# Two tiles of h made together, one small tile moved to another pool, and x1's transposes placed inside root's products

## The chip, the cores and the metric

The kernel runs on one core of a Trainium2 chip. The metric is the device time of one execution in microseconds (us); the kernel before takes 970.1 us (median of three runs, 969.67 to 971.27). TensorE is called PE, VectorE DVE, ScalarE ACT, GpSimd POOL; SP is the engine whose queue issues nearly all of the DMAs.

## The reference

Two graph layers over N = 625 nodes with D = 1024 features and E = 20,000 edges of R = 8 types, all in float32:

```python
# layer 0: attention over edges
h = x @ W
al, ar = h @ a[0, :d], h @ a[0, d:]
e = exp(-leaky_relu(al[src] + ar[dst], 0.1))
hp = segment_sum(e[:, None] * h[dst], src) / (segment_sum(e, src)[:, None] + 1e-5)
x = layernorm(x + elu(hp))
# layer 1: relational convolution with a gate
u = x @ root + bias
for r in range(8):
    sums, cnt = segment_sum(msgs of type r, dst), segment_sum(mask of type r, dst)
    u = u + (sums / max(cnt, 1)) @ weight[r]
z = concat([u, x]) @ w_gate + b_gate
x = layernorm(x + tanh(u) * z + x * (1 - z))
```

## The kernel before

The nodes are cut into ST = 5 tiles of 125 rows, the features into KC = 8 chunks of 128 or two halves of 512. All of it lies in one function, `fast` (L523); its order of instructions on each engine comes from a scheduler that goes by the program's order and by when operands are ready, except where `in_turn` (L561) pins an instruction to its place in the program. PSUM has eight banks, six in pool 0 and two in pool 1 (`bank`, L554).

**Layer 0.** SP loads the edge lists, x tile 0, the eight chunks of W (`load_w0`, L566), and x tile 1. POOL stores the packed edges to DRAM. `x_turned` (L717) turns a tile of x by eight PE transposes (px, L680) and ACT copies it (xT, L721). `h_parts` (L784) makes one tile of h: for each chunk two products (ph, L789), one per half, and at the end two ACT copies (h_sb, L793). Between tile 0's chunks stand `gather_edges` (L742: six small PE products, p_count, L746 and L747, then DVE's block numbers L749 and L751, and POOL's two gathers L755) and `place_edges` (L759: two PE transposes, p_edges, L763, and four DVE instructions that give keys and sources).

Then comes the counts stage. `one_hots` (L806, instructions L815) lets DVE compare keys and sources with a ramp; up to HOTS = 5 bundles of one-hots are held. For each of 55 groups `counts_of` multiplies them on PE (pc, L839) and ACT casts the counts (cj, L844); SP stores a tile's counts to DRAM (L900). The groups are interleaved with h of tiles 1 to 4 as steps of one chunk: 32 steps over the first H_GROUPS = 38 groups. A list `due` says after which group other work is issued: `row_sums` (L796, DVE's products L800, the attention's al and ar), `counted`, and `first_scores`, which begins with `spread_ar` (PE's p_ar, L930; ACT's copy L932). After the last group come the scores on DVE (L870 to L883), their transposes (patt, L891) and the products att times h (phh, L691). `attend` (L1089 on) makes x1 of a tile: elu, layernorm (scaled by ACT, L1111) and a store.

**Layer 1.** A float32 product is made of three: weights are cut into pieces g, m, e by ACT and DVE (`prepare`, L1014), x1 into pieces h, l, d (`turned_pieces`, L1040: eight transposes px, L680, then ACT L1035 and DVE L1036, L1037). `dense` (L1068) runs a weight half over the five tiles; in `dense_tiles` (L1045) a tile has sixteen first products (g times h L1051, m times l L1052) and eight second ones (e times d, L1055). For tile 0, and where two tiles go together, the second ones lie between the first ones; otherwise they follow. The two tiles 3 and 4 go together in root0 and root1. root0 is the first pass: after tile t's results are put, `later_x1(t)` calls `attend(t + 3)` and `turned_pieces(t + 2)`.

For each type r and half, `dense` gives y = x1 times weight, kept as two pieces in tiles of the pool f_y, and the neighbours' sum is 50 products pu (L1249): a 125 x 128 block of counts cf as weights, a piece of y with 512 columns moving. That makes 800 pu products in 16 blocks. `use_ins` (L1187) and `sum_ins` (L1196) use one small tile, in_p, 125 x 1, to check the number of edges; it lies in f_y behind inv, ahead of the y tiles. Layout in bytes of a partition: y tiles at 48,928 and on (288 modulo 512, each 2,048 long), cf at 77,184 (384 modulo 512). The pieces g, m, e, h, l, d are all at 384 modulo 512.

Of the kernel before, what the change touches and what calls it, by code (L numbers as in the profile page):

```python
# [10 lines left out]
F32 = mybir.dt.float32  # L11
# [11 lines left out]
KC = D // 128  # L23
# [417 lines left out]
ST = 5  # L441
TN = N // ST
# [80 lines left out]
def fast(  # L523
# [39 lines left out]
        tc.keep_in_program_order(ins)  # L563


    def load_w0(wpool):  # L566

        chunks = []
        for k in range(KC):
            if k % 2:  # L570
                w = rawp.tile([128, 2, HALF], F32, tag="raw", name=f"w0_{k}").rearrange("p i c -> p (i c)")
            else:
                w = wpool.tile([128, D], F32, tag="w", name=f"w0_{k}")
            nc.sync.dma_start(w, w0[k * 128:(k + 1) * 128, :])
            chunks.append(w)
        return chunks

    def load_row(rows, ap, name):
# [83 lines left out]
    def load_x(pool, t, name, bufs=None, eng=nc.sync, clear=False):  # L662

        xt = pool.tile([128, D], F32, tag="x", name=f"{name}_{t}", bufs=bufs)
        if t < ST - 1:
            eng.dma_start(xt, x[t * TN:t * TN + 128, :])
        else:
            if clear:
                nc.gpsimd.memset(xt[96:], 0.0)
            xr = x[t * TN:t * TN + rows_of(t), :]  # L670
            move_rows(rows_of(t), lambda rows: eng.dma_start(xt[rows], xr[rows]))
        return xt

    def transposed(src_t, n, name, put, pool=None):

        for g in range(2):
            p = bank(f"{name}_{g}", pool)
            for j in range(4):
                k = 4 * g + j
                nc.tensor.transpose(p[:, j * 128:j * 128 + n], src_t[:n, k * 128:(k + 1) * 128], ident[:n, :n])  # L680
            put(slice(4 * g, 4 * g + 4), p.rearrange("q (j n) -> q j n", j=4)[:, :, :n])

    banks_h = {}
# [11 lines left out]
    with tc.tile_pool(name="f_w", bufs=4, side="right") as wpool, \  # L695
# [10 lines left out]
        for i, ap in ((1, dst), (0, src), (2, etype)):  # L706
            nc.sync.dma_start(edge_rows[:, i, :], ap.rearrange("(p c) -> p c", c=per))
            if i == 1:
                x_next = load_x(xin, 0, "x")
        w0_sb = load_w0(wpool)  # L710
        nc.gpsimd.dma_start(packed[0:1, :], pad[:, :BLOCK])
        nc.gpsimd.dma_start(packed[NBLOCK + 1:, :].rearrange("(o i) c -> o (i c)", o=1), pad)
        x_next = [x_next, load_x(xin, 1, "x")]
        al_row = load_row(scores, a[0, :D], "al_row")
        ar_row = load_row(scores, a[0, D:], "ar_row")

        def x_turned(t):  # L717
            n = rows_of(t)
            xt = x_next.pop(0)
            xT = xin.tile([128, KC, 128], F32, tag="xT", name=f"xT_{t}")  # L720
            transposed(xt, n, f"px_{t}", lambda ks, p: nc.scalar.copy(xT[:, ks, :n], p), 0)  # L721
            if t + 2 < ST:
                x_next.append(load_x(xin, t + 2, "x"))
            return xT
# [17 lines left out]
        def gather_edges():  # L742

            p = bank("p_count", 0)
            for m in range(per // BLOCK):
                nc.tensor.matmul(p[:2 * NGS, :1], less[:, m, :], ones16[:TN], start=m == 0, stop=False)  # L746
            nc.tensor.matmul(p[:2 * NGS, :1], ahead16.rearrange("p g h -> p (g h)"), ones16[:1], start=False, stop=True)  # L747
            base = scores.tile([2 * NGS, 1], F32, name="base")
            nc.vector.tensor_copy(base, p[:2 * NGS, :1])  # L749
            at_block = scores.tile([2 * NGS, 2, 4], I32, name="at_block")  # L750
            nc.vector.tensor_scalar(at_block, later[:2 * NGS], base, float(NBLOCK + 1), op0=OP.add, op1=OP.min)  # L751
            edges = scores.tile([2 * NGS, 2, 4, BLOCK], F32, name="edges")
            for b in range(2):

                nc.gpsimd.indirect_dma_start(edges[:, b].rearrange("p i c -> p (i c)"), None, packed[:, :],  # L755
                                             bass.IndirectOffsetOnAxis(ap=at_block[:, b, :1], axis=0))
            return edges
# [25 lines left out]

        def h_parts(t, xT):  # L784
            n = rows_of(t)
            halves_h = [bank(f"ph_{t}_{half}", 1) for half in range(2)]
            for k in range(KC):
                for half, p in enumerate(halves_h):
                    nc.tensor.matmul(p[:n, :], xT[:, k, :n], w0_sb[k][:, half * HALF:(half + 1) * HALF],  # L789
                                     start=k == 0, stop=k == KC - 1)  # L790
                if k == KC - 1:
                    for half, p in enumerate(halves_h):
                        nc.scalar.copy(h_sb[:n, t, half * HALF:(half + 1) * HALF], p[:n, :])  # L793
                yield
# [104 lines left out]
            for r in range(R):  # L899
                nc.sync.dma_start(cd[r][:, :, j * 128:(j + 1) * 128], cj[:, :, r, :])  # L900

        for k, _ in enumerate(h_parts(0, xT_next)):
            if k == 0:
                edges = gather_edges()
            if k == KC - 2:
                place_edges()
        due = [(LAG, row_sums, 0)]
        cjs = []
        es = []

        def other_h():
            xT = x_turned(1)
            yield
            for t in range(1, ST):
                for k, _ in enumerate(h_parts(t, xT)):
                    if k == KC // 2 and t + 1 < ST:
                        xT_after = x_turned(t + 1)
                    yield
                xT = xT_after

        h_steps = other_h()
        next(h_steps)
        n_steps = (ST - 1) * KC
        steps = 0

        def spread_ar():
# [22 lines left out]
        for i in range(NGS):  # L949
            while steps < min(n_steps, (i + 1) * n_steps // H_GROUPS):  # L950
                next(h_steps, None)
                steps += 1
                if steps % KC == 0:
                    due.append((i + (LAG if steps < n_steps else 0), row_sums, steps // KC))
                    if steps == n_steps:
                        due.append((i + 6, first_scores, None))
            if i % NG == 0:
                cj = cjp.tile([128, ST, R, 128], F16, tag="cj", name=f"cj_{i // NG}")
                nc.gpsimd.memset(cj[:, :, :, TN:], 0.0)
                cjs.append(cj)  # L960
            n = built[i][2]
            if i == builds[n][0] and n + HOTS - 1 < len(builds):
                one_hots(n + HOTS - 1)
            counts_of(i, cjs[-1])
            if i % NG == NG - 1:
                due.append((i + LAG, counted, i // NG))
            due.sort(key=lambda d: d[0])
            while due and due[0][0] <= i:
                _, do, arg = due.pop(0)
                do(arg)  # L970
# [71 lines left out]
        h, l, d = x1[t] = [xp.tile([128, KC, 128], F32R, tag=f"{i}_{t}", name=f"{name}_{i}_{t}") for i in "hld"]  # L1042
        transposed(src_t, 128, f"p{name}_{t}", lambda ks, p: pieces_of(h, l, d, ks, p))

    def dense_tiles(ts, chunks, name, by_chunk):  # L1045

        sums = {t: (bank(f"p1_{name}_{t}"), bank(f"p2_{name}_{t}")) for t in ts}

        def first(t, k, g, m):
            h, l, _ = x1[t]  # L1050
            nc.tensor.matmul(sums[t][0], h[:, k, :], g, start=k == 0, stop=False, skip_group_check=True)  # L1051
            nc.tensor.matmul(sums[t][0], l[:, k, :], m, start=False, stop=k == KC - 1, skip_group_check=True)  # L1052

        def second(t, k, e):
            nc.tensor.matmul(sums[t][1], x1[t][2][:, k, :], e, start=k == 0, stop=k == KC - 1, skip_group_check=True)  # L1055

        for k, (g, m, e) in enumerate(chunks):
            for t in ts:
                first(t, k, g, m)
                if by_chunk:  # L1060
                    second(t, k, e)
        if not by_chunk:
            for k, (g, m, e) in enumerate(chunks):
                for t in ts:
                    second(t, k, e)
        return sums

    def dense(name, put, after=None, goes_on=False, whole=False):  # L1068

        chunks = [ready.pop(0) for _ in range(KC)]  # L1070


        steps = [(t,) for t in range(ST - 2)] + ([(ST - 2, ST - 1)] if goes_on else [(ST - 2,), (ST - 1,)])
        for ts in steps:
            for t, (p1, p2) in dense_tiles(ts, chunks, name, ts[0] == 0 or len(ts) > 1).items():
                n = 128 if whole else rows_of(t)
                put(t, p1[:n, :], p2[:n, :])
                if t == 1:
                    prepare(UNITS - KC)
                if after:  # L1080
                    after(t)
        prepare(2 * KC - UNITS)
# [78 lines left out]
                done.append(attend(t + 3))  # L1161
            turned_pieces(done[t + 2], t + 2, "x1")

    dense("root0", start_u(0), after=later_x1, goes_on=True, whole=True)
    elus.close()

    yp = ctx.enter_context(tc.tile_pool(name="f_y", bufs=1))
# [14 lines left out]
        for t in range(2, ST):  # L1182
            nc.vector.tensor_tensor(ins, ins16[:, t, :], ins, op=OP.add)

    in_p = yp.tile([TN, 1], F32, name="in_p")

    def use_ins():  # L1187
        p = bank("p_ins")
# [175 lines left out]
```

## Time and profile before

| what | before |
|---|---|
| runs | 970.1 us median (969.67 to 971.27) |
| profiled execution | 969.78 us, its span 968.0 us |
| granted PE clock | 0.995 of full speed on average |
| DVE, ACT, POOL busy | 596.6, 405.6, 36.5 us |
| PE px of x tile 0 | starts at 5.02 |
| first product of h | starts at 8.69 |
| first one-hot on DVE (L815) | 24.81 |
| last row sum on DVE ends | 104.08 |
| first phh | 111.14 |

The span runs from the first to the last instruction of the profiled execution; the remainder of its own time lies around it. A row of a timeline gives start, duration, engine, line and operation, output and inputs, the number of instructions joined in the row, and in brackets the idle time before them with what ended it. A row of PE's products counts the last one to its end, so that a row's duration is longer than the distance to the next row; the pitch is that distance over the number of products. Float32 products such as ph show two records each; pieces in the rounded form fp32r show one.

### The profile page before, as it was taken

To read this page: it belongs to the slowest core of one execution; us is meant where nothing else is said; L and a number is where in the kernel's file an instruction comes from. 1 tells how busy PE (TensorE), PEld (TensorE's weight loads), DVE (VectorE), ACT (ScalarE), POOL (GpSimd) and SP (SyncE) were. 2 spreads that over 40 slices of the span, in tenths; PEclk is the share of its full clock that TensorE was granted. 3 is DMA by queue.
4 is the path that set the end of the run, shared out by engine and by line. 5 is a ranking of instruction groups with operands and counts; after the bars stand their busy time and mean duration, and the time that the engine had idled before them with its cause. 6 is when DMAs were issued, how large, how long until landed. Compare 5 with 4: busy or idle time off the path is not lost.

```text
span 968.0 us, 10885 instructions
## 1 busy us (share of the span) xinstructions
PE 945.6 (98%) x4075; PEld 730.1 (75%) x4075; DVE 596.6 (62%) x964; ACT 405.6 (42%) x732; POOL 36.5 (4%) x59
## 2 busy tenths in 40 slices
PE   7999999999999999999999999999999999999994
PEld 3555546788888888888888888888888888888883
DVE  1998899853645737536356265363562654668996
ACT  1333857652452444415515434345243451435322
POOL 3000001000000000000000000000000000001123
PEclk9999999999999999999999999999999999999997
DMA  8123652341202213103021121220320211451213
GB/s 300 44 73 101 186 191 90 110 136 41 87 24 99 77 33 121 65 24 114 27 68 66 57 87 55 67 87 6 117 66 22 87 44 44 148 157 37 72 43 109
DMA packets 60479, 81.79 MB, mean 84 GB/s; under 512 B 29195, under 2 KB 29607, under 8 KB 60420
## 3 DMA queue, kind: packets, MB, share of 16 engines
q1 hardware_dynamic: 60212, 80.84, 26.3%
q8 instruction: 34, 0.56, 0.2%
q14 instruction: 25, 0.20, 0.1%
q0 software_dynamic: 208, 0.19, 0.1%
HBM read 69.26 MB, written 11.75 MB: 84 GB/s over the span
## 4 chain that ended last, share of the span: by engine, by line
PE 87%; DVE 8%; ACT 2%; issue 1%; POOL 1%; DMA 0%; SPq 0%; DVEq 0%; POOLq 0%; ACTq 0%
PE pu L1249 19%; PE p_w L1051 15%; PE p_w L1052 15%; PE p_w L1055 15%; PE ph L789 7%; PE p_wgx L1052 2%; PE p_wgx L1055 2%; PE p_wgx L1051 2%; PE pc L839 2%; PE p_root L1052 1%; PE p_root L1055 1%; PE p_root L1051 1%; PE p_wgu L1051 1%; PE p_wgu L1055 1%; PE p_wgu L1052 1%
## 5 line engine op out<-in xcount | busy, mean ns | idle before, releaser
L1051 PE MATMUL p_w<-g_w,x_h 128*128 128x512 f32 x640 | 249.2, 389 | 0.0
L1052 PE MATMUL p_w<-m_w,x_l 128*128 128x512 f32 x640 | 249.1, 389 | 0.0
L1249 PE MATMUL pu<-y,cf 125*128 125x512 f32 x800 | 189.8, 396 | 0.0
L1231 DVE SCALAR_TENSOR_TENSOR v<-p_w,v 125x512 f32<-125x512 f32 x80 | 55.2, 690 | 201.9 <-PE p_w L1055 155.7
L1249 PEld LDWEIGHTS pu<-y,cf 125*128 125x128 f32 x800 | 150.6, 188 | 36.4
L1055 PE MATMUL p_w<-e_w,x_d 128*128 128x512 f32 x640 | 176.3, 389 | 0.0
L1230 ACT ACTIVATE v<-p_w 125x512 f32<-125x512 f32 x80 | 47.5, 594 | 219.2 <-PE p_w L1052 206.7
L1051 PEld LDWEIGHTS p_w<-g_w,x_h 128*128 128x128 f32 x640 | 120.1, 188 | 25.2
L1052 PEld LDWEIGHTS p_w<-m_w,x_l 128*128 128x128 f32 x640 | 120.1, 188 | 25.0
L1055 PEld LDWEIGHTS p_w<-e_w,x_d 128*128 128x128 f32 x640 | 120.1, 188 | 25.0
L1024 DVE SCALAR_TENSOR_TENSOR m_w<-raw_w,e_w 128x512 fp32r<-128x512 f32 x128 | 85.1, 684 | 37.4 <-ACT e_w L1023 37.4
L1234 DVE TENSOR_TENSOR y<-v,y 125x512 fp32r<-125x512 f32 x80 | 55.3, 691 | 51.5 <-ACT y L1233 51.5
L1027 DVE TENSOR_TENSOR e_w<-g_w,m_w 128x512 fp32r<-128x512 f32 x128 | 85.0, 684 | 1.1
L1022 ACT ACTIVATE g_w<-raw_w 128x512 fp32r<-128x512 f32 x128 | 73.8, 620 | 24.3 <-PE p_w L1051 20.7
L1233 ACT CAST y<-v 125x512 fp32r<-125x512 f32 x80 | 49.1, 614 | 75.1 <-DVE v L1231 75.1
L789 PE MATMUL ph<-w,xT 128*125 128x512 f32 x160 | 77.7, 613 | 0.3 <-ACT xT L721 0.3
L1023 ACT ACTIVATE e_w<-raw_w 128x512 fp32r<-128x512 f32 x128 | 73.4, 619 | 0.0
L1253 DVE SCALAR_TENSOR_TENSOR u<-pu,inv,u 125x512 f32<-125x512 f32 x80 | 55.6, 741 | 5.2 <-PE pu L1249 5.2
L1213 ACT CAST cf<-cs 128x640 fp32r<-128x640 f16 x40 | 25.9, 724 | 50.0 <-PE pu L1249 48.6
L789 PEld LDWEIGHTS ph<-w,xT 128*125 128x125 f32 x160 | 27.9, 192 | 24.2 <-issue 22.3
L844 ACT CAST cj<-pc 128x480 f16<-128x480 f32 (+1 forms) x55 | 27.8, 557 | 41.2 <-PE pc L839 41.2
L691 PE MATMUL phh<-h_sb,attT 125*125 125x512 f32 x100 | 44.0, 593 | 0.5 <-DVE attT L896 0.5
(162 smaller groups left out, 979.6 us busy)
## 6 DMA issues: line engine op xcount, KB each, us to landing
raw_w<-in_L_gnn_weight_dram SPq DMA_DIRECT2D x64, 512.0 KB
cd<-cj SPq DMA_DIRECT2D x40, 160.0 KB
cs<-cd SPq DMA_DIRECT2D x8, 800.0 KB
x<-in_x_dram SPq DMA_DIRECT2D x8, 512.0 KB
w<-in_L_gnn_W_dram SPq DMA_DIRECT2D x8, 512.0 KB
raw_root<-in_L_gnn_root_dram SPq DMA_DIRECT2D x8, 512.0 KB
raw_wgx<-in_L_gnn_w_gate_dram SPq DMA_DIRECT2D x8, 512.0 KB
raw_wgu<-in_L_gnn_w_gate_dram SPq DMA_DIRECT2D x8, 512.0 KB
```

The source lines that it names most:

```text
L789: nc.tensor.matmul(p[:n, :], xT[:, k, :n], w0_sb[k][:, half * HALF:(half + 1) * HALF], start=k == 0, stop=k == KC - 1)
L1022: nc.scalar.activation(g, w, AF.Copy, scale=DOWN)
L1023: nc.scalar.activation(e, w, AF.Copy, scale=UP12 * DOWN)
L1024: rest = nc.vector.scalar_tensor_tensor(m, w, UP12, e.bitcast(F32), op0=OP.mult, op1=OP.subtract)
L1027: nc.vector.tensor_tensor(e, g.bitcast(F32), m.bitcast(F32), op=OP.subtract)
L1051: nc.tensor.matmul(sums[t][0], h[:, k, :], g, start=k == 0, stop=False, skip_group_check=True)
L1052: nc.tensor.matmul(sums[t][0], l[:, k, :], m, start=False, stop=k == KC - 1, skip_group_check=True)
L1055: nc.tensor.matmul(sums[t][1], x1[t][2][:, k, :], e, start=k == 0, stop=k == KC - 1, skip_group_check=True)
L1231: nc.vector.scalar_tensor_tensor(v[:n], p2, -EPS12, v[:n], op0=OP.mult, op1=OP.add)
L1234: nc.vector.tensor_tensor(lo[:n], v[:n], hi[:n].bitcast(F32), op=OP.subtract)
L1249: nc.tensor.matmul(p, c[:m, t, j * 128:(j + 1) * 128], piece[:m], start=(t == 0 and i == 0), stop=(t == ST - 1 and i == 1), skip_group_che ...
L1253: nc.vector.scalar_tensor_tensor(at, p[:n], inv[:n, j, r:r + 1], at, op0=OP.mult, op1=OP.add)
```

## The change

Three edits. **h**: x tile 1 is loaded right behind W's chunk 1; h of tiles 0 and 1 is made in step, chunk by chunk, after tile 0's chunk 0, the count, tile 0's chunk 1, tile 1's transposes and tile 1's chunks 0 and 1; the edges are placed at chunk 4 and tile 2 is turned at chunk 5. The remaining three tiles are 24 steps over the same 38 groups. Count products and tile 1's transposes are pinned in program order; h of tile 1 takes banks of pool 0. **in_p**: its tile comes from the pool `f_small`, which has four buffers and lies near the beginning of the left side; that moves the y tiles to byte 49,024 (384 modulo 512), while cf and the pieces stay. **root0**: `attend(t + 3)` and `turned_pieces(t + 2)` are called between a tile's first and second products and not after its results are put.

```diff
-    def load_w0(wpool):
+    def load_w0(wpool, after):
...
             chunks.append(w)
+            after(k)
...
-        w0_sb = load_w0(wpool)
+        w0_sb = load_w0(wpool, lambda k: k == 1 and x_next.append(load_x(xin, 1, "x")))
...
-                nc.tensor.matmul(p[:2 * NGS, :1], less[:, m, :], ones16[:TN], start=m == 0, stop=False)
+                in_turn(nc.tensor.matmul(p[:2 * NGS, :1], less[:, m, :], ones16[:TN], start=m == 0, stop=False))
...
-            halves_h = [bank(f"ph_{t}_{half}", 1) for half in range(2)]
+            halves_h = [bank(f"ph_{t}_{half}", 0 if t == 1 else 1) for half in range(2)]
...
-        for k, _ in enumerate(h_parts(0, xT_next)):
-            if k == 0:
-                edges = gather_edges()
-            if k == KC - 2:
+        two = [h_parts(0, xT_next)]
+        next(two[0])
+        edges = gather_edges()
+        next(two[0])
+        xT = x_turned(1, in_turn)
+        two.append(h_parts(1, xT))
+        for _ in range(2):
+            next(two[1])
+        for k in range(2, KC):
+            for parts in two:
+                next(parts)
+            if k == 4:
                 place_edges()
-        due = [(LAG, row_sums, 0)]
+            if k == 5:
+                xT = x_turned(2)
+        for parts in two:
+            next(parts, None)
+        due = [(LAG, row_sums, 0), (LAG + 2, row_sums, 1)]
...
-        n_steps = (ST - 1) * KC
+        h_steps = other_h(xT)
+        n_steps = (ST - 2) * KC
...
-    def dense_tiles(ts, chunks, name, by_chunk):
+    def dense_tiles(ts, chunks, name, by_chunk, between=None):
...
+        if between:
+            between(ts[0])
         if not by_chunk:
...
-    dense("root0", start_u(0), after=later_x1, goes_on=True, whole=True)
+    dense("root0", start_u(0), between=later_x1, goes_on=True, whole=True)
...
-    in_p = yp.tile([TN, 1], F32, name="in_p")
+    in_p = small.tile([TN, 1], F32, name="in_p")
```

## The prediction

> **What bounds the kernel now.** I read the page first: the span, the engines' shares, then the groups.
>
> ```profile
> span 968.0 us, 10885 instructions
> PE 945.6 (98%) x4075; PEld 730.1 (75%) x4075; DVE 596.6 (62%) x964; ACT 405.6 (42%) x732; POOL 36.5 (4%) x59
> ...
> L1051 PE MATMUL p_w<-g_w,x_h 128*128 128x512 f32 x640 | 249.2, 389 | 0.0
> ...
> L1249 PE MATMUL pu<-y,cf 125*128 125x512 f32 x800 | 189.8, 396 | 0.0
> ```
>
> PE is busy 945.6 of 968.0 us, so all its waits together, the start and the end included, are 22.4 us. To gain more, PE's own products must come closer together. The two groups hint at that: equal moving width, yet a pu product shows 396 ns and a p_w product 389. These means overlap one another; the pitch (distance between two starts) is what costs time. So the second view is PE's timeline around one w pass of layer 1:
>
> ```profile
> 268.11 0.39 PE L1051 MATMUL p_w<-g_w,x_h 128*128 128x512 f32 x1
> ...
> 273.55 0.39 PE L1051 MATMUL p_w<-g_w,x_h 128*128 128x512 f32 x1
> ...
> 284.43 11.86 PE L1249 MATMUL pu<-y,cf 125*128 125x512 f32 x50
> 296.13 0.39 PE L1051 MATMUL p_w<-g_w,x_h 128*128 128x512 f32 x1
> ```
>
> From 268.11 to 273.55 lie one tile's 24 products: 5.44 / 24 = 0.2267 us each. From 284.43 to 296.13 lie 50 pu products: 11.70 / 50 = 0.2340. There are 16 such blocks (8 types, 2 halves), and the chain of waits shows them all at 11.70. Third, PE's timeline of the start, and of root's first pass:
>
> ```profile
> 7.92 0.63 PE L746 MATMUL p_count<-ones,less 125*110 125x1 f16 x5 [1.00 <-DVE less L730]
> 8.47 0.24 PE L747 MATMUL p_count<-ones,ahead 1*110 1x1 f16 x1
> 8.69 14.03 PE L789 MATMUL ph<-w,xT 128*125 128x512 f32 x28
> 22.56 0.35 PE L763 MATMUL p_edges<-ident,edges 110*128 110x110 f32 x2
> ...
> 25.80 1.12 PE L789 MATMUL ph<-w,xT 128*125 128x512 f32 x2 [0.30 <-ACT xT L721]
> ```
>
> ```profile
> 178.31 0.50 PE L1055 MATMUL p_root<-e_root,x_d 128*128 128x512 f32 x1 [0.49 <-DVE x_d L1037]
> ...
> 180.13 0.73 PE L1052 MATMUL p_root<-m_root,x_l 128*128 128x512 f32 x2 [0.86 <-DVE x_l L1036]
> ```
>
> The brackets are what can be saved there: 0.30 and 0.49 + 0.86 = 1.35 us. Last, DVE's waits from 22 to 112 us, its slack in the counts stage:
>
> ```profile
> DVE attT L800 <- ACT h_sb L793: 4.4, 2, 4.1
> DVE s_hot L815 <- PE pc L839: 1.6, 2, 1.2
> DVE m_hot L815 <- PE pc L839: 1.4, 1, 1.4
> ```
>
> **Part 1, h.** PE has the same instructions as before, in another order. The six count products (L746, L747) took 7.92 to 8.69 = 0.77 us, beside PE's wait for W's chunk 0 (SP's next load, which waits on it, goes out at 8.57). Now they stand behind tile 0's chunk 0. The first product still waits for chunk 0, so they are paid: at least half of 0.77 at double clock, at most all. I take +0.6, nearer to all: the records of h stand 0.854 us apart until 12.23 and 0.429 afterwards, and chunk 0's four records end at 8.69 + 3.42 = 12.1. The wait of 0.30 for xT goes, since tile 0's next product covers tile 1's copies. Sum +0.3.
>
> The Trainium skill, "TensorE: Matmul & The Clock Gate", section "Part 1: The HAM clock gate", says the clock opens after a window of about 3.4 us that runs free of the kernel, so the point can vary by 0.5 us; the step at 12.23 agrees with about 3.4 us of work from 8.69, and by it this term could be 0.5 less or more.
>
> From rows, I let the sum reach from -0.3 (no count cost) to +0.8. W cannot take over as the wait: SP issues x tile 1 behind W's chunk 1, so chunks 2 to 7 land one transfer (1.27 us, the step of SP's issues at 8.57, 9.85, 11.12) later, while two tiles use a chunk in 2 x 4 x 0.429 = 3.43 us. The second load of root now goes out ahead of the cj_2 stores on SP, in the place of one load behind them; those stores (90.74 to 96.45) are needed by the first cast into cj_4 near 105, and 5.7 us of slack at most cover one load's issue. Nothing for it.
>
> What moves is DVE's start. p_edges now stands behind tile 0's chunk 0 (to 12.1), the count (0.6), tile 0's chunk 1 (4 x 0.429 = 1.72), tile 1's eight transposes (0.9), its chunks 0 and 1 (3.43), and chunks 2 to 4 of both tiles (3 x 3.43): 29.05, against 22.56, so 6.5 us later. DVE's chain from 22.95 to the end of the last row sum at 104.08 is 81.13 us with 73.40 busy, so 7.73 us are waits. Started at 29.4, with 0.3 of small gaps, it can end at 103.1, inside 104.08. The waits can shrink: 4.1 us of them are for h of tile 3, finished after step 24 of 32 (group 28) before and after step 16 of 24 (group 25) now; the others are for PE to give back one-hot buffers, so DVE was ahead. I take 0. Without that cover, every us is paid, at most 6.5: p_ar needs these sums.
>
> **Part 2, in_p.** A 4-byte tile moves from y's pool to the four-buffer pool at the start. Each buffer has 32 bytes: all on the left behind it moves by 128, y by 128 - 32 = 96, from byte 48,928 to 49,024, that is from 288 to 384 modulo 512. cf stays at 384, and p_w's x1 and weight pieces are at 384 before and after. No instruction changes and use_ins and sum_ins only read another address: the single effect is on pu's pitch. p_w (equal remainders) has 0.2267, pu (96 apart) 0.2340. What else differs is 125 rows for 128; but phh (L691, 125 rows) and ph (L789, 128 rows) both step by 0.429. That phh's remainders vary with the tile and its pitch doesn't speaks against the remainder, at least for plain f32 products, two passes of 0.429. In favour: pu's single steps repeat 238, 237, 231, 234, 235, 233, 232 ns with a period of 7, which fits neither the ten products of a sum nor the pairs of pieces; a cost of rows would be the same each time, while two streams of reads out of step would beat like this. I take p_w's row: 16 x (11.70 - 50 x 0.2267) = 16 x 0.365 = -5.8. Bounds: -5.9, and +3.2 if every step became the longest seen (800 x 0.004).
>
> The rule that speaks against: the Trainium skill, "SBUF — State Buffer", section "A bandwidth-pool intuition that's wrong (but worth ruling out)", gives PE a second, independent read port for weights. By it, where two operands lie is nothing to pu, the 0.0073 us have another cause, and the term is 0 (rival A); the trace shows a difference in pitch that this rule leaves unexplained.
>
> **Part 3, root0.** Tile 3's transposes reach PE 8 x 0.227 = 1.8 us earlier (168.2 for 169.99), so its pieces are cut before x1 of tile 4 is scaled, and not behind it (in ACT's timeline x_h at 175.75 comes right behind the scaling at 174.60). The stalls at 178.31 and 180.13 go: -1.35. But tile 4's transposes are due at 174.50 for 176.32, and x1 of tile 4 is ready at 174.60 + 1.25 = 175.85; that chain (DVE's stats to 173.08, POOL's rstd, ACT's shift and scaling) also shares DVE with tile 3's four pieces, 4 x 0.61 = 2.4 us, partly in DVE's idle 2.14. The new wait is 175.6 to 176.0 less 174.5 = 1.1 to 1.5. Then 8 second products (1.8 us) cover tile 4's pieces. Queued behind the waiting transposes are these products and the sums of tile 2, which nobody needs soon. Net: I take -0.1; between -1.35 (no new wait) and +0.5.
>
> **Sum.** The profiled execution's 969.78 us is 968.0 + 1.8 around it, 0.3 under the median 970.1. 969.78 + 0.3 - 5.8 - 0.1 = 964.2; carried to the median, **964.5 us**. With the small terms at both ends: 963.0 to 966.5.
>
> **Rivals.**
> A. The remainder does nothing to pu: the pitch stays 0.2340. For: phh's steady 0.429; the change touches no product. Against: the period of 7, and equal width at 0.2267. Time: 970.1 + 0.3 - 0.1 = 970.3.
> B. DVE becomes the bound of the counts stage. It starts 6.5 us later; if it wins back none of its 7.7 us of waits, the stage ends up to 6.5 us later and eats the gain: 964.5 + 6.5 = 971.0. It decides from 1 us on, when the waits that remain exceed 1.0 of 7.7. For: DVE is at 10.00 of 10 us from 30 to 60. Against: the waits are of a kind that a later start shortens. If about a third remain: 967.
> C. Slower: equal remainders are worse for pu, because its weights and its moving rows then start on the same place in each turn. Place: the 16 pu blocks; price at most +3.2 (0.238 throughout), 973.4 with the small terms; slower from a pitch above 0.2340, measurably from 0.2364. Against: p_w has equal remainders and the better pitch.
>
> **How the numbers follow.** The forecast has 0.76, A 0.12, B 0.08, C 0.04. A measurement tells 0.2% (1.9 us) from no change: under 968.2 is faster, over 972.0 slower. Faster: 0.76 and three quarters of B, 0.82. Same: A and the rest of B, 0.14. Slower: C, 0.04. The range runs from 963.0, the forecast's low end, to 970.8, which takes in A and nearly all of B; C, the rest of B and about 0.1 below 963.0 are left out.
>
> **What would show it.** Part 2: pu's blocks at 11.33 to 11.35 instead of 11.70 and steps of 226 and 227 without a period; 11.70 means A, more means C. Part 1: counts between chunk 0 and 1, no wait for xT, p_edges near 29, and patt at 109.8 + 0.3; a patt at 111 or later with DVE busy throughout means B. Part 3: no brackets at root0's last pair of tiles, one of 1.1 to 1.5 us ahead of the last px. The prediction is wrong if a block of pu keeps its length, or if DVE is waited for by more than 1 us ahead of p_ar.

## The result, and the profile after

The changed kernel takes 964.82 us (median of 4 runs, 963.90 to 964.96) against 970.55 (4 runs, 969.67 to 971.27): a ratio of 0.9939, 95% interval 0.9922 to 0.9957. The profiled execution takes 964.92 us, 4.9 less than the profiled one of before. Page of the changed kernel, whose lines have moved (pu is L1261, p_w's first product L1061):

```profile
span 963.1 us, 10881 instructions
PE 940.2 (98%) x4075; PEld 730.4 (76%) x4075; DVE 596.0 (62%) x964; ACT 404.5 (42%) x732; POOL 36.5 (4%) x59
...
L1061 PE MATMUL p_w<-g_w,x_h 128*128 128x512 f32 x640 | 249.4, 390 | 0.0
...
L1261 PE MATMUL pu<-y,cf 125*128 125x512 f32 x800 | 184.4, 389 | 0.0
```

Same number of PE instructions, PE's busy time 5.4 us down, the span 4.9 down: PE does the same work in less time, and its waits are half a microsecond longer. The group that changed is pu, 189.8 to 184.4. PE's timeline shows one of its blocks; from its start to the next p_w there are now 296.03 - 284.67 = 11.36 us, where there were 11.70:

```profile
284.67 11.52 PE L1261 MATMUL pu<-y,cf 125*128 125x512 f32 x50
296.03 0.40 PE L1061 MATMUL p_w<-g_w,x_h 128*128 128x512 f32 x1
```

All sixteen blocks are 11.36. PE's timeline of the start shows the new order, tile 0's chunk 0 and then the count:

```profile
8.42 3.75 PE L789 MATMUL ph<-w,xT 128*125 128x512 f32 x4 [1.82 <-DMA w<-in_L_gnn_W_dram]
11.96 0.58 PE L746 MATMUL p_count<-ones,less 125*110 125x1 f16 x5
12.47 0.24 PE L747 MATMUL p_count<-ones,ahead 1*110 1x1 f16 x1
12.64 2.62 PE L789 MATMUL ph<-w,xT 128*125 128x512 f32 x4
...
29.69 0.35 PE L763 MATMUL p_edges<-ident,edges 110*128 110x110 f32 x2
```

The count's products run from 11.96 to 12.64 with nothing to hide behind, and p_edges is at 29.69. DVE's waits from 22 to 112 us are shown next. Without the long first one, for p_edges, they have shrunk from 8.3 to 1.7 us:

```profile
DVE q L766 <- PE p_edges L763: 16.8, 1, 16.8
DVE e L870 <- ACT ar_b L942: 0.9, 1, 0.9
DVE s_hot L815 <- PE pc L839: 0.5, 1, 0.5
DVE attT L800 <- ACT h_sb L793: 0.3, 1, 0.3
```

And the transposes of x1's tiles 2, 3 and 4 in root0, on PE:

```profile
163.90 1.03 PE L681 MATMUL px<-ident,x 128*128 128x128 f32 x8
...
169.85 1.09 PE L681 MATMUL px<-ident,x 128*128 128x128 f32 x8 [1.27 <-ACT x L1123]
...
177.09 1.06 PE L681 MATMUL px<-ident,x 128*128 128x128 f32 x8 [0.68 <-issue]
```

There are two waits now, ahead of the transposes, 1.95 us together; the two behind them (1.35 us) are gone. For the second one the profile names no releaser ("issue").

Between the same events the two traces differ as follows (events are first products of their kind on PE; before, then after, then the difference):

| stretch | before | after | difference |
|---|---|---|---|
| start of the span to first phh | 111.14 | 111.41 | +0.27 |
| first phh to root0 | 46.94 | 46.94 | 0.00 |
| root0 and root1, to p_ins | 59.36 | 59.66 | +0.30 |
| p_ins to p_wgx (eight types) | 623.48 | 618.23 | -5.24 |
| p_wgx to the end of the span | 127.09 | 126.90 | -0.19 |

In the fourth row pu's sixteen blocks are together 5.45 us shorter (0.341 each), and the dense products 0.2 longer.

### The profile page after: what moved, and what is told of

Same layout as the page of the kernel before. It is cut to its first block, busy times and chain, and to the rows that moved or that the text cites. A ratio compares the mean times of both kernels' runs of the same rounds, so it can differ in the third digit from the quotient of the medians.

```text
span 963.1 us, 10881 instructions
## 1 busy us (share of the span) xinstructions
PE 940.2 (98%) x4075; PEld 730.4 (76%) x4075; DVE 596.0 (62%) x964; ACT 404.5 (42%) x732; POOL 36.5 (4%) x59
## 4 chain that ended last, share of the span: by engine, by line
PE 88%; DVE 7%; ACT 2%; issue 1%; POOL 1%; DMA 1%; SPq 0%; POOLq 0%; DVEq 0%; ACTq 0%
PE pu L1261 19%; PE p_w L1061 15%; PE p_w L1062 15%; PE p_w L1065 15%; PE ph L789 8%; PE p_wgx L1061 2%; PE p_wgx L1062 2%; PE p_wgx L1065 2%; PE p_root L1065 2%; PE pc L839 2%; PE p_root L1061 2%; PE p_root L1062 2%; PE p_wgu L1061 1%; PE p_wgu L1062 1%; PE p_wgu L1065 1%
## 5 line engine op out<-in xcount | busy, mean ns | idle before, releaser
L1061 PE MATMUL p_w<-g_w,x_h 128*128 128x512 f32 x640 | 249.4, 390 | 0.0
L1261 PE MATMUL pu<-y,cf 125*128 125x512 f32 x800 | 184.4, 389 | 0.0
L1261 PEld LDWEIGHTS pu<-y,cf 125*128 125x128 f32 x800 | 150.2, 188 | 31.6
L1061 PEld LDWEIGHTS p_w<-g_w,x_h 128*128 128x128 f32 x640 | 120.1, 188 | 25.2
L1314 POOL TENSOR_TENSOR u<-u,xr 125x512 f32<-125x512 f32 x10 | 14.2, 1417 | 747.9 <-ACT u L1299 726.9
```

The source lines that it names most:

```text
L1261: nc.tensor.matmul(p, c[:m, t, j * 128:(j + 1) * 128], piece[:m], start=(t == 0 and i == 0), stop=(t == ST - 1 and i == 1), skip_group_che ...
```

## The experiments

**The theory**: the place of y against cf sets pu's pitch, and is the whole gain. **The rivals**: the new order of work or the banks changed pu; or y has to lie at a certain place of its own. First each part by itself and in pairs.

In_p alone, on the kernel before:

```diff
-    in_p = yp.tile([TN, 1], F32, name="in_p")
+    in_p = small.tile([TN, 1], F32, name="in_p")
```

> The kernel before with nothing but in_p moved, so that y lies at 384 modulo 512 as cf does. Address theory: all sixteen pu blocks take 11.36 us as in the changed kernel, 16 x 0.34 = 5.4 us less than before, so about 965.0 us, slightly below the changed kernel, since its two other edits cost some 0.3 each by the traces. Rival (the order of the work or the banks made pu faster): blocks stay at 11.70 and the time at 970.5.

Measured 964.83 us (964.18 to 966.22) against 970.23, ratio 0.9941 (0.9926 to 0.9956). The blocks:

```profile
284.42 11.52 PE L1249 MATMUL pu<-y,cf 125*128 125x512 f32 x50
295.78 0.40 PE L1051 MATMUL p_w<-g_w,x_h 128*128 128x512 f32 x1
```

295.78 - 284.42 = 11.36. No instruction of this kernel differs from the one before, only addresses: the tiles on the left that lie behind in_p's new place move with y. The kernels below, one that moves y alone and one that moves cf, settle that it is y against cf.

The two other edits without it (the changed kernel with the line above put back):

> The changed kernel with in_p back in y's pool (y at 288). Address theory: blocks at 11.70, 970.5 + 0.3 (h) + 0.3 (root0) = 971.1 us. Rival: blocks at 11.36 and about 965.

Measured 969.87 us (12 runs, 968.42 to 971.07), ratio 0.9992 (0.9983 to 1.0001): no difference from before that can be told, where 971.1 was expected. The 0.3 us that a pair of traces puts on each small edit is not seen. The blocks are again 297.35 - 285.65 = 11.70:

```profile
285.65 11.86 PE L1261 MATMUL pu<-y,cf 125*128 125x512 f32 x50
297.35 0.39 PE L1061 MATMUL p_w<-g_w,x_h 128*128 128x512 f32 x1
```

So the order of the work is out as a cause of the shorter blocks, and in_p is the gain, as far as these times can tell. Then in_p with either small edit (root0's from the diff on the kernel before; the changed kernel with root0's call put back):

```diff
-    dense("root0", start_u(0), between=later_x1, goes_on=True, whole=True)
+    dense("root0", start_u(0), after=later_x1, goes_on=True, whole=True)
```

> in_p moved and the transposes inside root0's products, h as before. If root0's edit costs 0.3 as the traces compare, this is 0.3 above the kernel with in_p alone (965.3), with two waits of PE ahead of px in root0, about 1.3 and 0.7 us. Rival: root0 as forecast, 0.1 below in_p alone.

Measured 964.73 us (964.31 to 965.47): 0.1 below in_p alone, where 0.3 above was expected, although both waits are there (1.51 and 0.67 us).

> in_p moved and two tiles of h together, root0 as before. If h costs 0.3, this is 0.3 above in_p alone (965.3), with p_edges near 29.7 us, patt near 110.1 and only root0's old waits of 0.5 and 0.9 us. Rival: the h edit gains, below in_p alone.

Measured 963.91 us (963.08 to 965.05): 0.9 below in_p alone, where 0.3 above was expected.

**Which relation counts.** A kernel in which y walks over sixteen places:

```diff
+    y_all = agg.enter_context(tc.tile_pool(name="f_yall", bufs=1)).tile([128, 2 * ST * HALF + 128], F32R, name="y_all")
+    def y_at(n, off):
+        return y_all[:, off // 4 + n * HALF:off // 4 + (n + 1) * HALF]
...
-                hi, lo = (yp.tile([128, HALF], F32R, tag=f"y{i}_{t}", name=f"y{i}_{t}") for i in range(2))
+                hi, lo = (y_at(2 * t + i, 32 * (2 * r + h)) for i in range(2))
...
```

> The changed kernel with y's ten tiles as slices of one larger tile, whose start moves by 32 bytes with each of the sixteen passes (type, half): y minus cf modulo 512 is 0, 32, 64 to 480. The later tiles of the gate lie in a pool of their own. Address theory: the pitch of pu depends on the pass; 11.36 us a block at 0, 11.70 at 416 (which is -96), other values between or beyond, a smooth or a two-valued curve. Rival: one value for all sixteen.

Its first four blocks on PE, with the places 0, 32, 64 and 96:

```profile
246.19 11.52 PE L1265 MATMUL pu<-y_all,cf 125*128 125x512 f32 x50
257.55 0.40 PE L1061 MATMUL p_w<-g_w,x_h 128*128 128x512 f32 x1
...
284.77 11.82 PE L1265 MATMUL pu<-y_all,cf 125*128 125x512 f32 x50
296.43 0.40 PE L1061 MATMUL p_w<-g_w,x_h 128*128 128x512 f32 x1
...
323.64 11.62 PE L1265 MATMUL pu<-y_all,cf 125*128 125x512 f32 x50
335.11 0.39 PE L1061 MATMUL p_w<-g_w,x_h 128*128 128x512 f32 x1
...
362.36 11.83 PE L1265 MATMUL pu<-y_all,cf 125*128 125x512 f32 x50
374.03 0.39 PE L1061 MATMUL p_w<-g_w,x_h 128*128 128x512 f32 x1
```

In one kernel, with the same instructions, four blocks: 11.36, 11.66, 11.47, 11.67 us. Only the start of y differs between them. Mean pitch in ns of all sixteen blocks (block over 50), by the bytes from cf to y modulo 512:

```
  0 227.2    32 233.2    64 229.2    96 233.5   128 232.3   160 234.0   192 233.3   224 233.2
256 227.2   288 233.3   320 229.2   352 233.4   384 232.3   416 234.0   448 233.3   480 233.3
```

The second row repeats the first: at these steps of 32 bytes the remainder that counts is that of 256, not of 512. The place of before, 416, is with 160 the worst of these, and 64 would already have given most of the gain. This run took 968.79 us.

Next the other operand: the kernel before, y left at 288, cf moved there.

```diff
+    agg.enter_context(tc.tile_pool(name="gap", bufs=1, side="right")).tile([128, 24], F32, name="gap")
     aggp = agg.enter_context(tc.tile_pool(name="f_agg", bufs=1, side="right"))
```

> The kernel before with a gap of 96 bytes ahead of the counts' pool: y stays at 288 modulo 512, cf moves from 384 to 288 too. If the distance between the two operands decides: blocks at 11.36, 965.1 us. If y must lie at 384 itself: 11.70, 970.5.

Measured 965.32 us (964.90 to 967.68), ratio 0.9955 (0.9937 to 0.9973):

```profile
285.36 11.51 PE L1250 MATMUL pu<-y,cf 125*128 125x512 f32 x50
296.71 0.40 PE L1051 MATMUL p_w<-g_w,x_h 128*128 128x512 f32 x1
```

296.71 - 285.36 = 11.35 us. The distance decides, not the place itself.

Is it peculiar to pu? The changed kernel, with x1's pieces (the weights of every dense product) moved 96 bytes away from the moving g, m, e:

```diff
+    ctx.enter_context(tc.tile_pool(name="x1_gap", bufs=1, side="right")).tile([128, 24], F32, name="x1_gap")
     xp = ctx.enter_context(tc.tile_pool(name="f_x1", bufs=1, side="right"))
...
+    agg.enter_context(tc.tile_pool(name="gap", bufs=1, side="right")).tile([128, 104], F32, name="gap")
```

> The changed kernel with a gap of 96 bytes ahead of x1's pieces (and 416 more ahead of the counts, which stay at 384): x1's and later u's pieces, the weights of all dense products, lie at 288, the moving pieces g, m, e at 384. If the rule holds for every product of rounded float32 pieces: the dense products' pitch goes from 0.2267 to about 0.234 for 2,640 products, +19 us, near 984. If it is peculiar to pu: 965, pitches as in the changed kernel.

Measured 977.55 us, one run. One tile's second products to the next tile's:

```profile
267.36 2.02 PE L1066 MATMUL p_w<-e_w,x_d 128*128 128x512 f32 x8
...
272.96 2.02 PE L1066 MATMUL p_w<-e_w,x_d 128*128 128x512 f32 x8
```

5.60 / 24 = 0.2333 us, where it was 5.44 / 24 = 0.2267; pu's blocks stay at 11.36. So the rule holds for the dense products as well. The sum was expected at +19 and is +12.7 against the changed kernel. The pitch is that of +96 (233.5 in the table above), not the 234.0 of -96, so 2,640 x 0.0066 = 17.4 would be due, and from root0 to PE's last product the trace has 16.1. Against that stand 0.9 less ahead of phh and 2.6 less after PE's last product, which comes 10.8 us ahead of the span's end and not 13.4. Why that tail is shorter stays open.

Finer steps, as above with `4 * (2 * r + h)`:

> As the kernel with sixteen places, but with steps of 4 bytes: y minus cf is 0, 4, 8 to 60. The coarse steps gave 227.2 ns at 0, 233.2 at 32, 229.2 at 64, 232.3 at 128, the same again from 256 on. If reads go in units of 32 bytes or so, the values from 4 to 28 are like one another and like 32 (233) or worse, with units cut in two; if the beat depends on the exact distance, they differ from step to step, and one of them could be below 227. Time within 965 to 971 either way.

Measured 969.01 us. Mean pitch in ns by the bytes from cf to y:

```
 0 227.2    4 235.0    8 233.3   12 230.3   16 231.7   20 239.4   24 232.4   28 230.1
32 233.2   36 239.6   40 234.0   44 230.1   48 230.1   52 237.7   56 233.1   60 229.7
```

The block at 20 bytes, 451.64 - 439.67 = 11.97 us:

```profile
439.67 12.13 PE L1265 MATMUL pu<-y_all,cf 125*128 125x512 f32 x50
451.64 0.40 PE L1061 MATMUL p_w<-g_w,x_h 128*128 128x512 f32 x1
```

The values differ from step to step, so it is not a matter of whole units of 32 bytes; none is below that of 0.

**The small edits**, and one attempt at a better version, measured side by side. The new one starts `attend` one tile earlier:

```diff
-    for t in (1, 2):
+    for t in (1, 2, 3):
         done.append(attend(t))
...
-            if t + 3 < ST:
-                done.append(attend(t + 3))
+            if t + 4 < ST:
+                done.append(attend(t + 4))
```

> The changed kernel once more, beside the three others, to settle the small edits by times. If root0's edit costs 0.3 to 0.9, this is that much above the kernel with in_p and h alone: about 964.8 against 964.0.

> in_p and h, root0 as before. If the first reading holds (963.9 against 964.8 for in_p alone) h gains 0.9; if the traces' 0.3 of cost holds, this is 0.3 above in_p alone; if the first reading was scatter, the two agree within 0.3.

> in_p alone, for the comparison with the two others: 964.8 if the first reading holds, blocks of pu at 11.36.

> The changed kernel with attend of tile 3 ahead of root0 and tile 4's at the first call instead of the second. If x1's lateness makes root0's two new waits (1.27 and 0.68 us), they go and this gains up to 1.9 us against the changed kernel, near 963. Rival: DVE is the bound of this stretch (it has no idle time from 150 to 177 us), so the earlier work only makes the pieces of tiles 1 and 2 late: the waits come back there, within 0.5 of the changed kernel or slower.

| kernel | median us (range), side by side | median of all runs |
|---|---|---|
| in_p alone | 965.00 (964.77 to 965.54) | 964.91 of 11 |
| in_p and h | 964.11 (963.36 to 964.90) | 963.98 of 11 |
| in_p and root0 | | 964.73 of 6 |
| the changed kernel | 964.57 (963.85 to 964.90) | 964.72 of 9 |
| attend one tile earlier | 962.63 (962.14 to 963.92) | 962.63 of 5 |

With root0 as before, h gains 0.9 us both times. Root0's edit costs 0.7 on top of h and gains 0.2 without it; these are within the scatter of such medians, since runs of one kernel lie 1 to 2 us apart. In the profiles the stretch from root0 to p_ins is 59.36 or 59.37 us in five of six executions with the old root0 (59.69 in one), and 59.31 to 59.93 in six with the new one and the dense products at their usual place; the mean is 0.15 more. The new root0 gains nothing: its first wait is 0.89 to 1.51 us in these six, its second 0.66 to 0.68.

With attend one tile earlier the second wait is gone:

```profile
162.39 1.03 PE L681 MATMUL px<-ident,x 128*128 128x128 f32 x8
167.98 1.09 PE L681 MATMUL px<-ident,x 128*128 128x128 f32 x8 [0.91 <-ACT x L1123]
174.39 1.04 PE L681 MATMUL px<-ident,x 128*128 128x128 f32 x8
```

The stretch is 58.46 us, 0.85 less than the best with the new root0. The time came out as expected, the mechanism by half: the first wait stays (0.91, and 0.89 in the changed kernel's profile beside it), because x1 of tile 3 is ready no sooner. Its scaling on ACT ends 11.1 us behind root0's first product in both traces, that of tile 4 at 15.1 instead of 18.3. Why it is no sooner is not shown. The rival named DVE; but no wait came back at tiles 1 and 2, and DVE is not quite without idle time there (gaps of 0.56 and 0.65 us in the changed kernel).

The median is 1.9 below that of the changed kernel beside it; about 0.9 of this is shown by the stage. Where the remaining 1.0 lies is not shown: the two profiled executions also got to phh at 109.87 and 111.23 with the same instructions, but that is scatter of single executions. At 962.63, ratio to before 0.9926 (0.9912 to 0.9939), it is the best version of the study.

## Why the prediction was right, point by point

- **What bounds the kernel**: right. PE's share did not move, and the gain came from the pitch of products that nobody waited for.
- **in_p, -5.8**: the mechanism was right, and the size is -5.45. The pitch inside a block is 0.2267, as taken from p_w's row, but the first five steps after the change from p_w to pu are 233, 236, 228, 232 and 231 ns; these 26 ns more than five usual steps make 11.36 of the 11.33 foreseen. Rival A (the remainder does nothing) and rival C (equal remainders are worse) fell with in_p alone. Some distances do cost more than the old one, as C feared of equal remainders: 239.4 ns at 20 bytes and 239.6 at 36. So the best place could not be reckoned beforehand, only taken from a row that had it.
- The argument for A, phh's steady 0.429 whatever the remainder, did not carry over: plain float32 products and the rounded ones behave differently. The period of 7 in the steps was the telling sign: most of the coarse distances have a period of their own (at 192 and at 96 the steps repeat after three, 233, 233, 234 and 237, 231, 232), and at 0 there is only the rounding of 226.7. Its absence clears nothing: at 20 bytes nearly all steps are 240.
- The Trainium skill, "SBUF — State Buffer", section "A bandwidth-pool intuition that's wrong (but worth ruling out)", gives PE's weight loads a read port that is independent of the moving rows. The measurements differ: with the same instructions and sizes, and with each weight load (0.19 us) lying inside a step of pu (0.23), the distance of the two operands alone moves the pitch from 227.2 to 239.6 ns. Whatever the ports are, here the two streams are not independent. What they share I have not shown.
- **h, +0.3**: the sign is not borne out, and that the two profiled executions differ by +0.27 at phh is luck. At first the records of h stand 0.854 us apart, then 0.429; PE's granted clock goes to full in the traces at that point, 3.6 us behind h's first product in the trace of before and 5.5 us in that of the changed kernel. Counted against the later pace, the slow products lose 1.86 us before and 2.82 after. So +0.27 is made of a first product 0.27 earlier, 0.96 more lost on slow products, and an order of work that is 0.4 shorter.
- That 0.4 holds throughout. From h's first product to the first phh, without the loss on slow products, it is 100.2 us in all nine executions with the new order and 100.6 in three of five with the old one; in the other two (100.7 and 101.1) the edges' two transposes came 0.1 and 0.5 late. Three terms of the sum were off. The count, "I take +0.6, nearer to all", costs 0.44 at the later pace and 0.69 at the slow one. The wait for xT was worth more than 0.30: the step from px to the next product is 0.46 shorter and the one behind it 0.10. And the changes between counts and h were missed: the second record of h behind a count product comes 0.04 us late, and with two tiles of h ahead of the counts there are 24 such records instead of 31, -0.29. Together 0.44 - 0.56 - 0.29 = -0.4.
- The start itself scatters by more than that. In five executions with the old order the full clock came 3.3 to 5.5 us behind h's first product, and phh began between 110.89 and 112.40; with the new order h's first product itself began between 8.0 and 10.0 us, where it was 8.5 to 8.7. So the 0.9 that h gains beside the old root0 is more than the traces show, and why nothing of it is seen beside the new root0 stays open. The Trainium skill, "TensorE: Matmul & The Clock Gate", section "Part 1: The HAM clock gate", has the point of opening vary by 0.5 us either way; here it varied by 2.2 us in all.
- **DVE later by 6.5 us, at no cost**: right. p_edges came 7.1 us later; the waits fell from 8.3 us to 1.7 and the last row sum ended at 104.35 instead of 104.08. PE waits for nothing between its first product of h and the transposes patt at 110.08. It was close: hardly 0.8 us of waits that could still shrink are left, so by these rows rival B would begin with the next move in this direction; no run tried one.
- **root0, -0.1**: here a step failed, "Tile 3's transposes reach PE 8 x 0.227 = 1.8 us earlier (168.2 for 169.99)". PE was ready for them at 168.58, but x1 of tile 3 was scaled only from 168.57 to 169.80 on ACT (before: 168.02 to 169.25, in time for 169.99), so they began at 169.85. ACT's row of that scaling, before and after:

```profile
168.02 1.23 ACT L1111 ACTIVATE x<-x,shift,rstd 125x1024 f32<-125x1024 f32 x1
...
168.57 1.23 ACT L1123 ACTIVATE x<-x,shift,rstd 125x1024 f32<-125x1024 f32 x1
```

The prediction reckoned such a wait for tile 4 alone. Tile 4's wait came as said, ahead of the last px, but with 0.68 instead of 1.1 to 1.5: PE was there at 176.41 and not at 174.50, most of it through tile 3's wait, and x1 of tile 4 was scaled by 176.99 and not by 175.85. The bound of +0.5 held the profiled +0.30; over the six traces with the new root0 the stretch lies between 0.05 shorter and 0.57 longer than before.
- **The sum**: 964.5 against 964.82; in the profiled execution the terms are +0.27, -5.45, +0.30 and +0.2 of dense products that nobody foresaw, and -0.2 at the end. That the medians agree so closely is partly luck: in_p gave 0.35 less than reckoned and root0 nothing, while h's order gave 0.4 where a cost of 0.3 was reckoned. What is not luck is in_p, the term that decides.

## What to carry to other kernels

When PE is never idle, look at the distance between the starts of its products, and compare groups of equal width: a pitch that differs, and steps that repeat with a period that is not the program's, pointed here at where the operands lie. Keep weights (128 columns) and moving rows (512 columns) of rounded float32 products at the same place modulo 256 bytes, and after any change of a pool ahead of them check it: a tile of 4 bytes was worth 5.4 us here. And before work is moved forward on the busiest engine, ask of each piece of it when its input is ready, not only of the last one.

## What the runs showed of the hardware

- The pitch of fp32r products with 512 moving columns depends on the distance between the addresses of weights and moving operand: 227.2 ns at 0, 229 to 235 at most others, 239.4 and 239.6 at 20 and 36 bytes. At steps of 32 bytes it repeats after 256. Dense products do the same (226.7 at 0, 233.3 at +96).
- Moving both operands by 96 bytes changes nothing (11.35 and 11.36 us a block).
- phh, with plain float32 operands (attT's blocks start 500 bytes apart, h_sb's halves 2,048), stayed at 0.429 or 0.430 us between nearly all records in all of these kernels.
- The change from p_w to pu costs a few longer steps even at distance 0: five (26 ns) with all operands at 384, three (231, 232, 231) when y and cf lay at 288.
- The point from which PE's products of h took half the time moved by 2.2 us between five executions of the same instructions (3.3 to 5.5 us behind the first one), and what the slow products lose with it from 1.7 to 2.8 us; edits of a few tenths at the start can't be read from single traces.
